# Splitting the gate stage's second product for pairs of tiles into seven matmuls of 256 columns

## The chip, the cores and the metric

One core of a Trainium2 chip runs the kernel. The metric is the device time of one execution in microseconds. The kernel before took 3012.85 us (median of three runs, 3011.78 to 3013.1).

## What is computed

The input x has 4 sequences of 2048 tokens with 512 channels, in float32. It is normalized per token (xn), and the output is x + attention(xn) + ffn(xn).

```
shifted = pad(xn)[:, :-1]                         # the token before
xr, xk, xv = mu * xn + (1 - mu) * shifted         # one mu for each
r, k, v = xr @ Wr.T, xk @ Wk.T, xv @ Wv.T
wkv = recurrence over the tokens of a sequence(k, v, w, u), stabilized by a running maximum
attention = (sigmoid(r) * wkv) @ Wo.T
hidden = silu(xn @ W1.T) * (xn @ W3.T)            # 2048 hidden channels
ffn = fwht(hidden) @ W2.T                         # Walsh-Hadamard transform along the hidden axis
```

## The kernel before

The 8192 tokens are worked through in 8 blocks of 1024 (`TB`), number i from 0 to 7. Each block goes through three stages on TensorE (PE): the projections of k, v and r; the gate stage ("up": W1 and W3, 16 tiles j of 128 hidden channels); and the down stage (W2 and Wo together, with the transform folded into W2 in block 0). The recurrence (`wkv`, line 333) runs on VectorE (DVE) and ScalarE (ACT) meanwhile. It is cut into ten pieces for each of four heads of 128 channels. Each call of `step()` issues one piece: ten pieces lie in the projections, and every gate tile from 1 to 15 issues two. So pieces 1 and 2 of a head lie in tiles 1, 6 and 11, pieces 3 and 4 in tiles 2, 7 and 12, and so on to pieces 9 and 10 in tiles 5, 10 and 15.

Products of 2 x 2 blocks are done with seven products instead of eight (the scheme of Strassen and Winograd): the weights are cut into gate and linear rows and two halves of the channels, the tokens into two halves of 512. The seven weight forms of a tile are numbered 0 to 6. Each product contracts 256 channels, so it is two matmuls of 128 x 128 weights with 512 columns. Form 0 meets the first quarter b11 of xn, and form 4 meets t1 = b12 - b11, the first of the sums. All sums, on both sides, are made beforehand (`token_forms`, line 409, and `forms_in`, line 469), the weight forms in blocks 0 and 1 only; they are then kept in DRAM (`part_w`) and loaded for each tile into a ring of three buffers.

In blocks 1 to 7 the gate tiles 1 to 15 are issued by `up_pairs` (line 668), which runs two generators side by side, one step of each in turn. `up_rest` (line 566) does one tile: products f1 (form 4 on t1), f2 (form 5), m21 (form 1), f3 (form 3), m22 (form 6) and f4 (form 2). PE accumulates in PSUM banks, and between the products ACT copies a bank into another that goes on from the same partial sum: pc from pb after f2, pd from pb after f3. The product f1 has a bank of its own, pf, which ACT copies into the buffer s5, in SBUF; DVE adds s5 to pb and pc (lines 606 and 608). The gate's nonlinearity is a tanh on ACT and two multiplications on DVE for each half of the tokens; for the second half they are the tail, which is issued in the middle of the next tile, after f2 and the copy into pc.

For tiles 4 to 15 the form 0 product is done for two tiles at once. Two tiles, two blocks of 128 channels and two quarters of 256 tokens make another 2 x 2, so `pair_product` (line 630) does seven matmuls of 256 columns where two tiles would have four of 512. It is run in the even tile two before its pair, in two banks a and b. Its matmuls, numbered by form, stand among the products of that tile like this: f1, P1, f2, P0, m21, P2, f3, P4 P5 P3, m22, P6, f4. ACT copies a part of one bank into the other between them (b<-a after P0, a<-b after P2, b<-b after P5) and the first product into `pair_s5`. At the end of the tile `out` (line 640) empties a and b into `pair_out`: ACT copies the lower 256 columns, DVE adds `pair_s5` to the upper ones. From `pair_out`, `fill` (line 559) copies twice, into the banks pb and pa of each tile of the pair; it does so one tile ahead, just before that earlier tile's f4.

What sets the order: every engine works its instructions in the order of the program (`InOrder`, line 26), and waits stand on its own queue. The eight banks are a queue in the gate stage: `take()` gives the one that has been free longest, `give()` appends. The order of the down stage is written out by hand (`down`, line 955). It starts with the banks that are free then, and uses the three of the last tile's tail, sorted by number, for another set; of these, ACT clears the third (`d0.clear("f")`, line 1018) once the tail has read it. The tail of tile 15 and the last pieces of the recurrence are issued in `before()`, line 1014. The first matmuls of the down stage are three groups of five with 256 columns.

Loads of weights are issued by SyncE (SP), in the order of the program. `normalize_early` (line 222) normalizes the next block during the gate stage, in three slots of 1024 columns in `pieces_w`.

Of the kernel before, what the change touches and what calls it, by code (L numbers as in the profile page):

```python
# [10 lines left out]
F32 = mybir.dt.float32  # L11
AF = mybir.ActivationFunctionType
ALU = mybir.AluOpType
# [3 lines left out]
P = 128  # L17
H = 512
TB = 2 * H
# [22 lines left out]
def tile_rwkv_attn_hadamard_ffn(  # L42
# [37 lines left out]
    down_w = dram.tile([2, 7, KH, P, QR, P], F32, name="down_w")  # L80
    deep_w = dram.tile([7, 7, P, QR, P], F32, name="deep_w")

    pair_w = dram.tile([NF // 2, P, 7, P], F32, name="pair_w")
    stat_d = dram.tile([n_blocks, 2, TB], F32, name="stat_d")
    xn_d = dram.tile([C, TB], F32, name="xn_d")

# [14 lines left out]
    def unit(j):  # L101
        return right[:, j // NP, j % NP, :]
# [20 lines left out]
    def take():  # L123
        return free_banks.popleft()

    def give(*pts):
        free_banks.extend(pts)
# [3 lines left out]
    tf_flat = tf.rearrange("p f k t -> p (f k t)")  # L131
    x_first, x_tok = (flat.rearrange("p (t c) -> p t c", c=C) for flat in (k_flat, tf_flat))

    pair_sums = k_sb[:, 0, :].rearrange("p (n t) -> p n t", n=4)
    pair_out = v_sb[:, 0, :].rearrange("p (n t) -> p n t", n=2)
    pair_s5 = unit(NF - 1)[:, 0 : H // 2]

    pair_forms = pieces_w[:, 7].rearrange("p q c -> p (q c)")[:, 0 : 4 * P].rearrange("p (f c) -> p f c", f=4)
    spread = v_sb[:, 0:2, :]
    stage = [v_sb[:, 2 + s // 2, ts(s % 2, H)] for s in range(4)]  # L140
    u2_of = [e1b[:, ts(g, H)] for g in range(KH)]
# [80 lines left out]
    def normalize_early(i):  # L222

        flat = pieces_w.rearrange("p u q c -> p (u q c)")
        both = flat[:, 0 : 2 * TB].rearrange("p (s t) -> p s t", t=TB)
        slots = [flat[:, ds((2 + n) * TB, TB)] for n in range(3)]

        def load(b):
            sp.dma_start(out=slots[b % 3], in_=xT[ts(b, P), ds(i * TB, TB)])

        load_spread(i, both)
        for b in range(3):
            load(b)
        yield
        for b in range(NB):
            xb = slots[b % 3]
            for s, op in ((0, ALU.mult), (1, ALU.add)):
                dve.tensor_tensor(xb, xb, both[:, s, :], op)
                if s:
                    sp.dma_start(out=xn_d[ts(b, P), :], in_=xb)  # L240
                    if b + 3 < NB:
                        load(b + 3)
                yield


# [215 lines left out]
    def seven_forms(t, a11, a12, a22, a21):  # L461

        sub = ALU.subtract
        pool.tensor_tensor(t[1], a21, a22, ALU.add)
        pool.tensor_tensor(t[2], t[1], a11, sub)
        pool.tensor_tensor(t[3], a12, t[2], sub)
        pool.tensor_tensor(t[0], a11, a21, sub)
# [4 lines left out]
    def load_parts(i, chunk):  # L472
        kind, n = chunk
        t = ring_a.tile([P, 7, KH, P], F32, tag="a", name=f"part_{i}_{kind}_{n}")
        if kind == "pair":
            sp.dma_start(out=t.rearrange("p f k c -> p (f k) c")[:, 0:7], in_=pair_w[n])
        elif kind == "rest":
            sp.dma_start(out=t[:, 1:7], in_=part_w[n][:, 1:7])
        elif is_first(i, n):
            sp.dma_start(out=t[:, 0:4], in_=wpart[n])  # L480
            forms_in(t)
        else:
            sp.dma_start(out=t, in_=part_w[n])
        return t

    def make_pair(p, w0, w1):
        (a11, a12), (a21, a22) = ([w[:, 0, b] for b in range(KH)] for w in (w0, w1))
        seven_forms([pair_forms[:, n] for n in range(4)], a11, a12, a22, a21)
        sp.dma_start(out=pair_w[p][:, 0:2], in_=w0[:, 0])
        sp.dma_start(out=pair_w[p][:, 2], in_=w1[:, 0, 1])  # L490

    def keep_pair(p):
        sp.dma_start(out=pair_w[p][:, 3:7], in_=pair_forms)

    def is_first(i, n):
        return i == (1 if n < 3 * KH else 0)
# [59 lines left out]

    def fill(row):

        pb, pa = take(), take()
        act.copy(pb, pair_out[:, row])
        act.copy(pa, pair_out[:, row])
        return pa, pb

    def up_rest(key, j, w, filled, tail, step, then):

        m11, m21, m22, f1, f2, f3, f4 = right_of["up"]
        h0, h1 = unit(j)[:, 0:H], unit(j)[:, H:TB]

        def product(pt, form, right, start=False):
            for b in range(KH):
                pe.matmul(
                    pt, lhsT=w[:, form, b, :], rhs=right[:, b, :], start=start and b == 0, stop=b == KH - 1,
                    skip_group_check=True,
                )

        if filled:
            pa, pb = filled
        else:  # L580
            pa, pb = take(), take()
            product(pa, 0, m11, True)
            act.copy(pb, pa)
        pf = take()
        product(pf, 4, f1, True)
        s5 = small.tile([P, H], F32, tag="s5", name=f"s5_{key}")
        act.copy(s5, pf)
        give(pf)
        yield
        product(pb, 5, f2)  # L590
        pc = take()
        act.copy(pc, pb)
        for f in tail:
            f()
        yield
        product(pa, 1, m21)
        act.activation(h0, pa, AF.Tanh, scale=0.5)
        yield
        product(pb, 3, f3)
        dve.scalar_tensor_tensor(h0, h0, 1.0, pa, ALU.add, ALU.mult)  # L600
        give(pa)
        pd = take()
        act.copy(pd, pb)
        yield
        step()
        dve.tensor_tensor(pb, pb, s5, ALU.add)
        product(pc, 6, m22)
        dve.tensor_tensor(pc, pc, s5, ALU.add)
        yield
        then()  # L610
        step()
        product(pd, 2, f4)
        yield (
            lambda: act.activation(h1, pc, AF.Tanh, scale=0.5),
            lambda: dve.tensor_tensor(h0, h0, pd, ALU.mult),
            lambda: dve.scalar_tensor_tensor(h1, h1, 1.0, pc, ALU.add, ALU.mult),
            lambda: dve.tensor_tensor(h1, h1, pb, ALU.mult),
            lambda: give(pd, pc, pb),
        )

    def pair_quarters():
        return [b11[:, b, cols] for b in range(KH) for cols in (lo, hi)]

    def make_pair_sums():
        q11, q12, q21, q22 = pair_quarters()
        t1, t2, t3, t4 = (pair_sums[:, n] for n in range(4))
        for out, x, y in ((t1, q12, q11), (t2, q22, t1), (t3, q22, q12), (t4, q21, t2)):
            difference(out, x, y)

    def pair_product(w):  # L630

        w = w.rearrange("p f k c -> p (f k) c")
        q11, _, q21, q22 = pair_quarters()
        t1, t2, t3, t4 = (pair_sums[:, n] for n in range(4))
        a, b = take(), take()

        def matmul(n, pt, right, start=False):
            pe.matmul(pt, lhsT=w[:, DEEP_AT[n]], rhs=right, start=start, stop=True, skip_group_check=True)

        def out(row, pt):  # L640
            act.copy(pair_out[:, row, lo], pt[:, lo])
            dve.tensor_tensor(pair_out[:, row, hi], pt[:, hi], pair_s5, ALU.add)


        matmul(1, a[:, hi], t1, True)
        act.copy(pair_s5, a[:, hi])
        yield
        matmul(0, a[:, lo], q11)
        act.copy(b[:, hi], a[:, lo])
        yield  # L650
        matmul(2, b[:, hi], t2)
        act.copy(a[:, hi], b[:, hi])
        yield
        matmul(4, a[:, lo], q21)
        matmul(5, b[:, hi], t3)
        act.copy(b[:, lo], b[:, hi])
        matmul(3, a[:, hi], q22)
        yield
        matmul(6, b[:, lo], t4)
        yield  # L660
        out(0, a)
        out(1, b)
        give(a, b)
        yield

# [1 line left out]

    def up_pairs(i, chunk, tail, step, beside):

        filled = None  # L670
        for j in range(1, NF):
            w = chunk(2 if j % 2 and j > 1 else 1)
            beside(j)
            ahead = []

            def fill_next():
                if 2 * FIRST_PAIR <= j + 1 < NF:
                    ahead.append(fill((j + 1) % 2))

            rest = up_rest(f"{i}_{j}", j, w, filled, tail, step, fill_next)  # L680
            product = iter(())
            for n in range(6):
                left = next(rest)
                if n == 0 and j % 2 == 0 and j + 2 < NF:
                    product = pair_product(chunk(0))
                next(product, None)
            tail, filled = left, ahead[0] if ahead else None
        return tail
# [546 lines left out]
    for i in range(n_blocks):  # L1235
# [34 lines left out]
        def chunk(more):  # L1270

            for _ in range(more):
                if loaded[0] < len(order):
                    parts.append(load_parts(i, order[loaded[0]]))
                    loaded[0] += 1
            return parts.pop(0)
# [70 lines left out]


        if i:
            make_pair_sums()  # L1350
            tail = up_pairs(i, chunk, tail, step, lambda j: staging(i, j))
        for j in range(NF if i == 0 else 0):
            if j % 2 and j > 2 * FIRST_PAIR:
# [95 lines left out]
```

## Time and profile before

| | |
|---|---|
| time, median of three | 3012.85 us |
| profiled execution, its own time | 3011.08 us |
| its span, first to last instruction | 3009.3 us |
| granted TensorE clock | 1.000 |
| gate stage of one block (1250 to 1430 us): busy PE, DVE, ACT | 180.0, 146.3, 93.0 of 180 us |
| DMA, mean over the span | 146 GB/s |

Busy time is the union of the instructions of an engine. The chain of waits follows the work that ended last back to its beginning; its pieces carry the start, the duration and the engine. In timelines each matmul of this kernel's program appears as two records, and a line such as "x12" merges twelve records of one kind; an idle time in front, and the engine that ended it, stand in brackets. Nearly all instructions carry line 36, that of `InOrder`, so they are told apart by their tiles: `right` holds the gate tiles and r, `part_rest` and `part_pair` are weights of the gate stage, `pieces_w` those of the down stage, `s` is s5, `v_sb` holds `pair_out`, `k_sb` the pair's sums, and `e`, `e1b`, `sa`, `sb` belong to the recurrence.

### The profile page before, as it was taken

The numbers are of one execution on the slowest core, as the hardware profiler recorded it, in microseconds if no ns is written. First come the engines' busy times: TensorE is split into PE (matmuls) and PEld (weight loads), VectorE is DVE, ScalarE is ACT, GpSimd is POOL, SyncE is SP. The second block draws the span as 40 slices with busy tenths as digits, with TensorE's granted clock in tenths as the row PEclk, the third lists the DMA queues.
The fourth block names the chain that finished last, engine by engine and source line by source line (L and its number), as shares of the span: only waits on it lengthen the run. The fifth ranks groups of instructions, "written<-read, shape, count | busy, mean of one in ns | idle before, by whom it ended". The sixth has DMA issues, their size and how long they took to land.

```text
span 3009.3 us, 26145 instructions
## 1 busy us (share of the span) xinstructions
PE 2993.2 (99%) x8954; PEld 1699.2 (56%) x8954; DVE 2428.0 (81%) x2637; ACT 1266.0 (42%) x2328; POOL 230.5 (8%) x220
## 2 busy tenths in 40 slices
PE   8999999999999999999999999999999999999999
PEld 3444444448644486445854558545585446844568
DVE  7688547789878897788977889778887788877887
ACT  4334134553345523554235542455425454144441
POOL 4264012220000000000000000000000000000000
PEclk9999999999999999999999999999999999999999
DMA  4266523666423374233633336332463324622244
GB/s 177 90 222 226 220 88 126 225 231 234 139 102 112 110 235 134 103 113 115 231 120 121 106 142 210 116 119 96 158 202 118 121 99 136 203 96 74 92 141 150
DMA packets 154979, 440.22 MB, mean 146 GB/s; under 512 B 16352, under 2 KB 36320, under 8 KB 152672
## 3 DMA queue, kind: packets, MB, share of 16 engines
q1 hardware_dynamic: 154560, 437.97, 42.6%
q8 instruction: 72, 1.18, 0.2%
q10 hardware_dynamic: 288, 0.59, 0.1%
q14 instruction: 59, 0.48, 0.0%
HBM read 363.01 MB, written 75.49 MB: 146 GB/s over the span
## 4 chain that ended last, share of the span: by engine, by line
PE 92%; DVE 7%; ACT 1%; DMA 0%; issue 0%; SPq 0%; DVEq 0%; ACTq 0%
PE bank L36 92%; DVE e1b L36 3%; DVE right L36 2%; DVE bank L36 1%; DVE e L36 1%; DVE v_sb L36 0%; ACT bank L36 0%; DMA xnT<-xT 0%; DVE sa L36 0%; ACT right L36 0%; DVE sb L36 0%; SPq L36 0%; DVE xnT L36 0%; DVE tf L36 0%; DVEq L1445 0%
## 5 line engine op out<-in xcount | busy, mean ns | idle before, releaser
L36 ACT COPY bank<-bank 128x512 f32<-128x512 f32 (+1 forms) x701 | 344.2, 491 | 999.1 <-PE bank L36 956.8
L36 PE MATMUL bank<-right,pieces_w 128*128 128x256 f32 (+1 forms) x2928 | 736.4, 409 | 2.9 <-ACT bank L36 2.9
L36 PEld LDWEIGHTS bank<-right,pieces_w 128*128 128x128 f32 x2928 | 555.1, 190 | 173.1 <-issue 99.2
L36 PE MATMUL bank<-tf,part_rest 128*128 128x512 f32 x1344 | 611.3, 592 | 1.6 <-ACT bank L36 1.6
L36 PEld LDWEIGHTS bank<-tf,part_rest 128*128 128x128 f32 x1344 | 255.1, 190 | 279.3 <-issue 248.3
L36 PE MATMUL bank<-right,part_full 128*128 128x512 f32 x840 | 369.6, 593 | 0.0
L36 DVE SCALAR_TENSOR_TENSOR right<-right,bank 128x512 f32<-128x512 f32 x256 | 175.1, 684 | 240.1 <-ACT right L36 239.4
L36 DVE TENSOR_TENSOR right<-right 128x1280 f32<-128x1280 f32 (+2 forms) x236 | 327.7, 1414 | 13.0 <-PE bank L36 12.0
L36 PE MATMUL bank<-tf,part_full 128*128 128x512 f32 x704 | 324.8, 592 | 0.0
L36 PE MATMUL bank<-xnT,part_rest 128*128 128x512 f32 x672 | 315.8, 592 | 0.0
L36 PEld LDWEIGHTS bank<-right,part_full 128*128 128x128 f32 x840 | 158.4, 190 | 203.2 <-issue 183.9
L36 ACT ACTIVATE right<-bank 128x512 f32<-128x512 f32 x308 | 184.1, 600 | 155.7 <-PE bank L36 110.2
L36 PE MATMUL bank<-xnT,part_full 128*128 128x512 f32 x528 | 248.1, 592 | 0.0
L36 PEld LDWEIGHTS bank<-tf,part_full 128*128 128x128 f32 x704 | 133.8, 190 | 159.4 <-issue 149.7
L36 DVE RECIPROCAL e1b<-e1b 128x512 f32<-128x512 f32 x64 | 213.9, 3343 | 0.0
L36 DVE TENSOR_TENSOR bank<-bank,s 128x512 f32<-128x512 f32 x256 | 168.2, 691 | 42.3 <-PE bank L36 29.8
L36 PEld LDWEIGHTS bank<-xnT,part_rest 128*128 128x128 f32 x672 | 127.7, 190 | 130.9 <-issue 117.2
L36 DVE TENSOR_TENSOR right<-right,bank 128x512 f32<-128x512 f32 x256 | 173.9, 679 | 6.5 <-PE bank L36 2.0
L36 PEld LDWEIGHTS bank<-xnT,part_full 128*128 128x128 f32 x528 | 100.3, 190 | 117.8 <-issue 113.3
L36 ACT COPY s<-bank 128x512 f32<-128x512 f32 x128 | 74.5, 582 | 214.0 <-PE bank L36 213.0
L36 PE MATMUL bank<-k_sb,pieces_w 128*128 128x256 f32 x630 | 146.3, 379 | 0.0
L36 DVE SCALAR_TENSOR_TENSOR right<-xnT,vec,right 128x1024 f32<-128x1024 f32 x92 | 121.9, 1355 | 21.3 <-ACT right L36 21.3
(137 smaller groups left out, 3160.3 us busy)
## 6 DMA issues: line engine op xcount, KB each, us to landing
pieces_w<-deep_w SPq DMA_DIRECT2D x343, 320.0 KB, 3.1
part_rest<-part_w SPq DMA_DIRECT2D x84, 768.0 KB, 4.3
part_full<-part_w SPq DMA_DIRECT2D x64, 896.0 KB, 4.6
part_w<-part_full SPq DMA_DIRECT2D x22, 896.0 KB, 6.7
part_pair<-pair_w SPq DMA_DIRECT2D x42, 448.0 KB, 4.1
pieces_w<-down_w SPq DMA_DIRECT2D x56, 320.0 KB, 4.7
deep_w<-pieces_w SPq DMA_DIRECT2D x7, 2240.0 KB, 8.6
tf<-x SPq DMA_DIRECT2D x7, 2048.0 KB, 7.9
```

What stands on the lines that cost most here:

```text
L36: return self.tc.keep_in_program_order(issue(*args, **kwargs))
```

## The change

In blocks 2 to 7 the form 4 product is done for pairs of tiles as well. `pair_product` gets a number: 0 is the product on b11 (form 0), run in the even tile as before, and 1 is the product on t1 (form 4), run in the odd tile just before its pair. Its results go not to `pair_out` but straight to the two s5 buffers of the coming pair, to which `up_rest` copied pf until now. For tiles 4 to 15 of these blocks `up_rest` issues no f1, takes no bank pf and makes no copy. Block 1 keeps f1.

Around it: the sums of t1's quarters are made by DVE at tile 2 of each block, into the place of tile 14. The weight forms of the second pair product are made by GpSimd (POOL) in block 0, beside those of the first, and kept in DRAM; in the other blocks SP loads them, at the even tile, into columns of `pieces_w` that were the third slot of `normalize_early`, which is left with two.

```diff
@@ normalize_early
-        slots = [flat[:, ds((2 + n) * TB, TB)] for n in range(3)]
+        slots = [flat[:, ds((2 + n) * TB, TB)] for n in range(2)]
...
@@ make_pair, keep_pair
-        (a11, a12), (a21, a22) = ([w[:, 0, b] for b in range(KH)] for w in (w0, w1))
-        seven_forms([pair_forms[:, n] for n in range(4)], a11, a12, a22, a21)
-        sp.dma_start(out=pair_w[p][:, 0:2], in_=w0[:, 0])
-        sp.dma_start(out=pair_w[p][:, 2], in_=w1[:, 0, 1])
+        for n, form in enumerate((0, 4)):
+            (a11, a12), (a21, a22) = ([w[:, form, b] for b in range(KH)] for w in (w0, w1))
+            seven_forms([pair_forms[n][:, m] for m in range(4)], a11, a12, a22, a21)
+            sp.dma_start(out=pair_w[n, p][:, 0:2], in_=w0[:, form])
+            sp.dma_start(out=pair_w[n, p][:, 2], in_=w1[:, form, 1])
...
-        sp.dma_start(out=pair_w[p][:, 3:7], in_=pair_forms)
+        for n in range(2):
+            sp.dma_start(out=pair_w[n, p][:, 3:7], in_=pair_forms[n])
@@ up_rest
-        pf = take()
-        product(pf, 4, f1, True)
-        s5 = small.tile([P, H], F32, tag="s5", name=f"s5_{key}")
-        act.copy(s5, pf)
-        give(pf)
+        if s5 is None:
+            pf = take()
+            product(pf, 4, f1, True)
+            s5 = small.tile([P, H], F32, tag="s5", name=f"s5_{key}")
+            act.copy(s5, pf)
+            give(pf)
@@ pair_product
-        def out(row, pt):
-            act.copy(pair_out[:, row, lo], pt[:, lo])
-            dve.tensor_tensor(pair_out[:, row, hi], pt[:, hi], pair_s5, ALU.add)
+        def out(slot, pt):
+            act.copy(slot[:, lo], pt[:, lo])
+            dve.tensor_tensor(slot[:, hi], pt[:, hi], s5, ALU.add)
...
-        out(0, a)
-        out(1, b)
+        for slot, pt in zip(outs(), (a, b)):
+            out(slot, pt)
@@ up_pairs
+            if i >= 2 and j == 2:
+                make_pair_sums(1)
...
+            def new_s5():
+                s5_pair[:] = [small.tile([P, H], F32, tag="s5", name=f"s5_{i}_{2 * pair + row}") for row in range(2)]
+                return s5_pair
...
+            both = i >= 2 and pair >= FIRST_PAIR
...
-                if n == 0 and j % 2 == 0 and j + 2 < NF:
-                    product = pair_product(chunk(0))
+                if n == 0 and pair >= FIRST_PAIR and 2 * pair < NF:
+                    if j % 2 == 0:
+                        product = pair_product(0, chunk(0).rearrange("p f k c -> p (f k) c"), kept)
+                        if both:
+                            sp.dma_start(out=pair_w1, in_=pair_w[1, pair])
+                    elif both:
+                        product = pair_product(1, pair_w1, new_s5)
```

More of the change, by code (lines that the diff above doesn't have):

```diff
@@ L81, in tile_rwkv_attn_hadamard_ffn @@
     deep_w = dram.tile([7, 7, P, QR, P], F32, name="deep_w")
-    pair_w = dram.tile([NF // 2, P, 7, P], F32, name="pair_w")
+    pair_w = dram.tile([2, NF // 2, P, 7, P], F32, name="pair_w")
     stat_d = dram.tile([n_blocks, 2, TB], F32, name="stat_d")
@@ L132, in tile_rwkv_attn_hadamard_ffn @@
     x_first, x_tok = (flat.rearrange("p (t c) -> p t c", c=C) for flat in (k_flat, tf_flat))
-    pair_sums = k_sb[:, 0, :].rearrange("p (n t) -> p n t", n=4)
+    pair_sums = [t.rearrange("p (n t) -> p n t", n=4) for t in (k_sb[:, 0, :], unit(NF - 2))]
     pair_out = v_sb[:, 0, :].rearrange("p (n t) -> p n t", n=2)
-    pair_s5 = unit(NF - 1)[:, 0 : H // 2]
-    pair_forms = pieces_w[:, 7].rearrange("p q c -> p (q c)")[:, 0 : 4 * P].rearrange("p (f c) -> p f c", f=4)
+    pair_s5 = [unit(NF - 1)[:, ts(n, H // 2)] for n in range(2)]
+    pair_w1 = pieces_w.rearrange("p u q c -> p (u q c)")[:, ds(4 * TB, 7 * P)].rearrange("p (f c) -> p f c", f=7)
+    pair_forms = [
+        t[:, 0 : 4 * P].rearrange("p (f c) -> p f c", f=4)
+        for t in (pieces_w[:, 7].rearrange("p q c -> p (q c)"), k_sb[:, 0, :])
+    ]
     spread = v_sb[:, 0:2, :]
@@ L225, in normalize_early @@
         both = flat[:, 0 : 2 * TB].rearrange("p (s t) -> p s t", t=TB)
-        slots = [flat[:, ds((2 + n) * TB, TB)] for n in range(3)]
+        slots = [flat[:, ds((2 + n) * TB, TB)] for n in range(2)]
         def load(b):
-            sp.dma_start(out=slots[b % 3], in_=xT[ts(b, P), ds(i * TB, TB)])
+            sp.dma_start(out=slots[b % 2], in_=xT[ts(b, P), ds(i * TB, TB)])
         load_spread(i, both)
-        for b in range(3):
+        for b in range(2):
             load(b)
@@ L235, in normalize_early @@
         for b in range(NB):
-            xb = slots[b % 3]
+            xb = slots[b % 2]
             for s, op in ((0, ALU.mult), (1, ALU.add)):
@@ L240, in normalize_early @@
                     sp.dma_start(out=xn_d[ts(b, P), :], in_=xb)
-                    if b + 3 < NB:
-                        load(b + 3)
+                    if b + 2 < NB:
+                        load(b + 2)
                 yield
@@ L475, in load_parts @@
         if kind == "pair":
-            sp.dma_start(out=t.rearrange("p f k c -> p (f k) c")[:, 0:7], in_=pair_w[n])
+            sp.dma_start(out=t.rearrange("p f k c -> p (f k) c")[:, 0:7], in_=pair_w[0, n])
         elif kind == "rest":
@@ L564, in fill, with up_rest @@
         return pa, pb
-    def up_rest(key, j, w, filled, tail, step, then):
+    def up_rest(key, j, w, filled, s5, tail, step, then):
         m11, m21, m22, f1, f2, f3, f4 = right_of["up"]
@@ L619, in up_rest, with pair_quarters, make_pair_sums, pair_product @@
         )
[L621 to L626, printed above, removed]
+    def pair_quarters(n):
+        return [(b11, t1)[n][:, b, cols] for b in range(KH) for cols in (lo, hi)]
+    def make_pair_sums(n):
+        q11, q12, q21, q22 = pair_quarters(n)
+        t1, t2, t3, t4 = (pair_sums[n][:, m] for m in range(4))
         for out, x, y in ((t1, q12, q11), (t2, q22, t1), (t3, q22, q12), (t4, q21, t2)):
             difference(out, x, y)
[L630 to L634, printed above, removed]
+    def pair_product(which, w, outs):
+        q11, _, q21, q22 = pair_quarters(which)
+        t1, t2, t3, t4 = (pair_sums[which][:, m] for m in range(4))
+        s5 = pair_s5[which]
         a, b = take(), take()
@@ L638, in matmul @@
             pe.matmul(pt, lhsT=w[:, DEEP_AT[n]], rhs=right, start=start, stop=True, skip_group_check=True)
-        def out(row, pt):
-            act.copy(pair_out[:, row, lo], pt[:, lo])
-            dve.tensor_tensor(pair_out[:, row, hi], pt[:, hi], pair_s5, ALU.add)
+        def out(slot, pt):
+            act.copy(slot[:, lo], pt[:, lo])
+            dve.tensor_tensor(slot[:, hi], pt[:, hi], s5, ALU.add)
         matmul(1, a[:, hi], t1, True)
-        act.copy(pair_s5, a[:, hi])
+        act.copy(s5, a[:, hi])
         yield
@@ L668, in up_pairs, with kept @@
     def up_pairs(i, chunk, tail, step, beside):
-        filled = None
+        filled, s5_pair = None, [None, None]
+        def kept():
+            return [pair_out[:, row] for row in range(2)]
         for j in range(1, NF):
@@ L673, in up_pairs @@
             beside(j)
-            ahead = []
+            if i >= 2 and j == 2:
+                make_pair_sums(1)
+            ahead, pair = [], j // 2 + 1
             def fill_next():
@@ L678, in fill_next @@
                     ahead.append(fill((j + 1) % 2))
-            rest = up_rest(f"{i}_{j}", j, w, filled, tail, step, fill_next)
+            def new_s5():
+                s5_pair[:] = [small.tile([P, H], F32, tag="s5", name=f"s5_{i}_{2 * pair + row}") for row in range(2)]
+                return s5_pair
+            rest = up_rest(f"{i}_{j}", j, w, filled, s5_pair[j % 2], tail, step, fill_next)
             product = iter(())
+            both = i >= 2 and pair >= FIRST_PAIR
             for n in range(6):
                 left = next(rest)
-                if n == 0 and j % 2 == 0 and j + 2 < NF:
-                    product = pair_product(chunk(0))
+                if n == 0 and pair >= FIRST_PAIR and 2 * pair < NF:
[5 more added lines that the diff above has]
+                        product = pair_product(1, pair_w1, new_s5)
                 next(product, None)
@@ L1349, in tile_rwkv_attn_hadamard_ffn @@
         if i:
-            make_pair_sums()
+            make_pair_sums(0)
             tail = up_pairs(i, chunk, tail, step, lambda j: staging(i, j))
```

## The prediction, made before the change was run

> **What bounds the kernel now.** I read the shares of busy time and the chain first, then the chain in order of time, then the timelines of TensorE (PE), VectorE (DVE) and ScalarE (ACT) over one block, 1242 to 1440 us. (Blocks 1 to 7 repeat every 368.6 us: the chain shows the same sequence at 1038.84, 1407.41 and 1775.98.)
>
> ```profile
> PE 2993.2 (99%) x8954; PEld 1699.2 (56%) x8954; DVE 2428.0 (81%) x2637; ACT 1266.0 (42%) x2328; POOL 230.5 (8%) x220
> ...
> PE 92%; DVE 7%; ACT 1%; DMA 0%; issue 0%; SPq 0%; DVEq 0%; ACTq 0%
> ```
>
> PE has no idle time to win; less PE work is the only way to go faster. But the chain spends 24 us per block on DVE:
>
> ```profile
> 1407.41 0.57 ACT bank L36
> 1407.98 0.52 ACT right L36
> 1408.53 0.70 DVE right L36
> ...
> 1430.80 0.66 ACT bank L36 x2
> 1431.50 344.46 PE bank L36 x1072
> ```
>
> ```profile
> 1424.38 6.79 PE L36 MATMUL bank<-right,pieces_w 128*128 128x256 f32 x30
> 1431.50 2.43 PE L36 MATMUL bank<-right,pieces_w 128*128 128x256 f32 x10 [0.33 <-ACT bank L36]
> ```
>
> Here, where the gate stage ends and the down stage starts, PE waits, although only 0.33 us: DVE runs without a gap from 1408.53 to there, finishing the last head of the recurrence. So PE and DVE are both at their limit at the end of each block, and PE work taken out in front of this point returns as waiting.
>
> **The gain.** The timeline shows each of the program's matmuls as two records, so starts give the price:
>
> ```profile
> 1365.12 0.59 PE L36 MATMUL bank<-k_sb,part_pair 128*128 128x256 f32 x2
> 1365.56 0.59 PE L36 MATMUL bank<-xnT,part_pair 128*128 128x256 f32 x2
> ...
> 1368.14 5.31 PE L36 MATMUL bank<-tf,part_rest 128*128 128x512 f32 x12
> 1373.29 1.88 PE L36 MATMUL bank<-xnT,part_rest 128*128 128x512 f32 x4
> ```
>
> 256 columns take 0.43 us, 512 columns 5.15/6 = 0.858 us. A pair loses four of 512 (3.43 us) and gains seven of 256 (3.01): 0.42 us less. Blocks 2 to 7 have six such pairs each: 36 x 0.42 = 15.2 us. A rule speaks against this: the Trainium skill, "TensorE: Matmul & The Clock Gate", section "Back-to-back issue gap", gives streams of weight load and matmul about 81 ns at 128 columns and 131 ns at 512, so narrow matmuls cost more than their share. Drawn straight between, 256 columns would cost 0.75 of 512 (an estimate from that page), and a pair 7 x 0.64 - 3.43 = +1.05 us, 38 us in all. The row has exactly half, with the weight load (190 ns) beside it, so I take the row.
>
> **What is added elsewhere.** ACT, per pair: two copies of 512 go (2 x 0.58), six of 256 come (6 x 0.37): +1.1 us, on an engine 52% busy in this stage (93 of 180 us). DVE: two additions of 256 per pair (2 x 0.41), and four differences per block (1.7 us), which lie in the 3.4 us that DVE idles early in tile 2 (before 1265.57). SP: one load of 448 KB more per pair, 0.32 us to issue, 4.1 us to land, issued a tile (11.6 us) ahead and behind a part load that has to wait for the tile's start anyhow: nothing. Normalizing ahead with two slots instead of three: a load now waits for the store from its slot, but is needed five tiles (58 us) later: nothing; were that cover gone, some 5 us of DVE per block. Block 0: POOL makes 24 forms more, 2.6 us per pair (rows of 1.11, 0.60, 0.46, 0.45), and SP issues three stores more per pair; POOL is at most 67% busy there, and forms are made two tiles ahead: 0, at most 2 us in all.
>
> **Middle of the block: a wait that moves.** Without the first-sum product a tile is, on PE: P1, f2, P0, m21, P2, f3, P4 P5 P3, m22, P6, f4 = 11.6 us, where each P is one pair matmul of 256 columns, and each other name a product of two matmuls of 512. A tile's start is now where the previous f4 ends, and f2 ends 2.15 us later, instead of 3.43 or more. After f2 ACT has, in this order, the copy into pc, the tanh of the last tile, and the copy b<-a that P2 needs:
>
> ```profile
> 1384.27 0.57 ACT L36 COPY bank<-bank 128x512 f32<-128x512 f32 x1 [1.34 <-PE bank L36]
> 1384.76 0.60 ACT L36 ACTIVATE right<-bank 128x512 f32<-128x512 f32 x1
> 1385.24 0.39 ACT L36 COPY bank<-bank 128x256 f32<-128x256 f32 x1
> ```
>
> These take 1.36 us (1384.27 to 1385.63), and P2 comes 2.15 us after f2's end: the copy into pc may start at most 2.9 us into the tile. In every pair tile after the change pc is the bank that the pair product of the tile before calls b, and the copy waits for the DVE addition that empties it. That addition stands behind the tile's two pieces of recurrence. The trace has this case with its whole length, in tile 10 (f4 ends at 1369.86), whose pieces are the two longest:
>
> ```profile
> 1363.98 3.34 DVE L36 RECIPROCAL e1b<-e1b 128x512 f32<-128x512 f32 x1
> ...
> 1373.17 0.75 DVE L36 TENSOR_TENSOR v_sb<-bank,right 128x256 f32<-128x256 f32 x2
> ```
>
> It ends at 1373.92, 4.06 us into the next tile. Before, tile 11 had no pair product, so only ACT waited (1.32 us, with the tanh behind it). After: pc copy at 4.17, b<-a done at 5.53, P2 at 5.59 instead of 4.29: 1.3 us of PE idle. Tiles 5 and 10 carry these pieces, so tiles 6 and 11 pay; tile 9 now also has additions, which adds about 0.1 in tile 10 and 0.1 in tile 11. Elsewhere, by the same walk: after the pieces of tiles 3 and 8 the addition ends at 2.5, after 4 at 2.7, after the light ones at 1.3 to 2.2: no stall. Sum 1.3 + 0.1 + 1.4 = 2.8 us per block, 16.8 in six. Bounds: 2.0 to 3.6 per block (12 to 22), as the 2.9 limit is missed or met by 0.1 to 0.2 in four tiles.
>
> **End of the block.** From the end of m21 of tile 13 (1398.62) to the resume at 1431.50 the trace takes 32.88 us; PE could have resumed after 15 products of two matmuls of 512, 25.74, and 15 matmuls of 256, 6.45: 32.2. So 0.68 us are lost before (by starts; the idle of 0.33 is counted from the modelled end). After: two first-sum products (14 and 15) go, 3.43, and P2 to P6 of tile 13's new product come, 2.15: PE is ready at 30.9. DVE has no such relief: its order from tile 13's gate multiplication on is the same, plus tile 13's two additions, 0.67: its last operation ends 33.9 us after m21 (before: 1432.08 - 1398.62 = 33.46; 0.67 more, and 0.2 of waiting goes). And PE waits for a later one of its operations. ACT must clear a bank of the last tile before the copy that frees PE:
>
> ```profile
> 1430.08 0.68 DVE L36 TENSOR_TENSOR right<-right,bank 128x512 f32<-128x512 f32 x1
> 1430.68 0.68 DVE L36 SCALAR_TENSOR_TENSOR right<-right,bank 128x512 f32<-128x512 f32 x1
> 1431.39 0.69 DVE L36 TENSOR_TENSOR right<-right,bank 128x512 f32<-128x512 f32 x1
> ```
>
> Before, it is the bank read by the first of these three (ended 1430.76, clear at 1430.80). It is the last by number of the tail's three banks, and the new rotation makes it the bank of the third row in five blocks and of the second in one. From the end of that operation to PE the trace has 0.74. So PE resumes at 33.9 + 0.74 = 34.7: idle 3.8, loss 3.1 us; in the one block 2.4. In all 5 x 3.1 + 2.4 = 17.9 us. Bounds per block: 1.8, if the clear waited for the first of the three rows as before, to 3.8, the whole idle: 11 to 23.
>
> **Sum.** -15.2 + 16.8 + 17.9 = +19.5 us. The profiled execution took 3011.08 us (span 3009.3), 1.8 us under the median of 3012.85; I add the difference to the median: 3032. Range of this case from the bounds: -15 + 12 + 11 = +8 to -15 + 22 + 23 + 2 = +32: 3021 to 3045.
>
> **Rivals.**
> - The full gain arrives, 2998 us: PE stays without gaps. For it: PE 99% busy, ACT 52%, DVE 81% in the stage (146 of 180 us from 1250 to 1430). Against: at the end of each block PE already waits for DVE, and this cannot hold unless DVE's last operation came 3 us earlier relative to PE. Decisive is a single point, the resume after the first three down products; if its idle stays at 0.33 us and P2 never waits, this rival is right. 0.07.
> - Only one of the two places pays. Block ends alone: -15.2 + 17.9, 3016; P2 alone: -15.2 + 16.8, 3014. For the first: the pc copy could find its bank empty earlier if DVE gets ahead. Both give a time that nothing tells from no change. 0.15.
> - Dearer than I count: a stall in more tiles (the 2.5 to 2.7 cases pass the 2.9 limit by little), or narrow matmuls that cost more beside 512-column neighbours: 0.3 us in eight more tiles per block gives +14, 3046. The rows show no such price. 0.10.
> - The likeliest, 3032 (3021 to 3045): 0.68.
>
> A measurement of this kernel tells about 0.2% (6 us) from no change. Faster by more: 0.08; within: 0.14; slower: 0.78. To hold 8 in 10 the range takes in the likeliest case and most of the second: 3013 to 3043.
>
> **What would show it.** After: PE idle "<-ACT bank" in front of P2 in tiles 6 and 11 of blocks 2 to 7, about 1.3 us; ACT's pc copy waiting for DVE there, on `s` or `v_sb`; an idle of some 3.5 us at the first down product that resumes, preceded in the chain by DVE's recurrence; block 1 unchanged, blocks 2 to 7 some 3.2 us longer each. I am wrong if the blocks get shorter, if idle stands in front of f2 or m22 (ACT's fill), or if PE shows no idle but matmuls of 256 start more than 0.43 us apart.

## The result and the profile after

The changed kernel took 3038.48 us (median of four runs, 3037.04 to 3038.61), against 3012.97 for the kernel before: a ratio of 1.0084, with a 95% interval of 1.007 to 1.0099. One of the four runs of the kernel before that were taken beside it is a slow one of 6501.43 us, whose cause is not known: the ratio leaves it out, and the other three took 3011.78 to 3013.1. The predicted 3032 us is 6.5 us short, and the time lies in the range of 3013 to 3043. The profiled execution took 3038.53 us, its span 3036.6.

The page of the changed kernel, first the busy time of the engines (share of the span, number of instructions), then the chain by engine:

```profile
PE 2987.4 (98%) x9170; PEld 1736.4 (57%) x9170; DVE 2464.3 (81%) x2733; ACT 1293.5 (43%) x2472; POOL 251.9 (8%) x244
...
PE 80%; DVE 18%; ACT 2%; issue 0%; DMA 0%; ACTq 0%; DVEq 0%
```

PE is busy for 5.8 us less and the span is 27.3 us longer. (Busy time is no measure of the work taken out: a start that is late without an idle counts as busy.) In the chain DVE rose from 7 to 18%: PE now waits for it more often. One group of the page shows the same (busy, mean ns, idle in front and its releaser), before and after. It holds the down products on `right`, and after the change the second pair product's matmuls on t1's sums too, since these lie in `right` and their weights in `pieces_w`:

```profile
L36 PE MATMUL bank<-right,pieces_w 128*128 128x256 f32 (+1 forms) x2928 | 736.4, 409 | 2.9 <-ACT bank L36 2.9
```

```profile
L36 PE MATMUL bank<-right,pieces_w 128*128 128x256 f32 (+1 forms) x3216 | 824.0, 407 | 26.9 <-ACT bank L36 26.9
```

The chain of the changed kernel over one block, in order of time (start, duration):

```profile
1434.94 1.23 DVE e L36
1436.16 1.21 DVE bank L36 x2
1437.37 1.13 DVE right L36
1438.53 2.43 DVE right L36 x3
1441.68 230.44 PE bank L36 x780
...
1685.27 3.26 DVE e1b L36
...
1693.23 1.22 DVE right L36
1696.63 35.37 PE bank L36 x102
```

Before, PE carried the chain from one block end to the next (344 us in one piece). Now it goes over to DVE in the middle as well, and PE resumes at 1696.63. What PE does there, in its timeline (in brackets the idle in front, and what ended it):

```profile
1691.41 1.88 PE L36 MATMUL bank<-tf,part_rest 128*128 128x512 f32 x4
1693.12 0.59 PE L36 MATMUL bank<-xnT,part_pair 128*128 128x256 f32 x2
1693.55 1.88 PE L36 MATMUL bank<-xnT,part_rest 128*128 128x512 f32 x4
1696.63 0.70 PE L36 MATMUL bank<-k_sb,part_pair 128*128 128x256 f32 x2 [1.19 <-ACT bank L36]
1697.16 1.88 PE L36 MATMUL bank<-tf,part_rest 128*128 128x512 f32 x4
```

This is tile 6: f2, P0, m21, and then P2, which was due at 1693.55 + 1.72 = 1695.27 and starts 1.36 us late. The step after it takes 0.53 us instead of 0.43. The cause stands in the timelines of DVE and ACT:

```profile
1693.23 1.22 DVE L36 SCALAR_TENSOR_TENSOR right<-right,e1b 128x1024 f32<-128x1024 f32 x1
1694.38 0.75 DVE L36 TENSOR_TENSOR s<-bank,right 128x256 f32<-128x256 f32 x2
```

```profile
1695.21 0.57 ACT L36 COPY bank<-bank 128x512 f32<-128x512 f32 x1 [2.40 <-DVE s L36]
1695.69 0.60 ACT L36 ACTIVATE right<-bank 128x512 f32<-128x512 f32 x1
1696.18 0.39 ACT L36 COPY bank<-bank 128x256 f32<-128x256 f32 x1
```

The copy into pc waits 2.40 us for the DVE additions that empty tile 5's pair banks; these stand behind piece 10 of the recurrence, whose last operation starts at 1693.23. The tanh and b<-a follow, and only then P2. Tile 11 has the same, with v_sb in the place of s (ACT waits 3.23 us there) and the same 1.19 us of idle on PE.

The end of the block, PE first, then ACT, then DVE's three tail rows:

```profile
1804.35 4.48 PE L36 MATMUL bank<-right,pieces_w 128*128 128x256 f32 x20
1810.43 2.42 PE L36 MATMUL bank<-right,pieces_w 128*128 128x256 f32 x10 [1.60 <-ACT bank L36]
1814.51 2.43 PE L36 MATMUL bank<-right,pieces_w 128*128 128x256 f32 x10 [1.65 <-ACT bank L36]
```

```profile
1809.51 0.60 ACT L36 ACTIVATE right<-bank 128x512 f32<-128x512 f32 x1 [6.91 <-DVE bank L36]
1810.00 0.38 ACT L36 COPY bank<-bank 128x256 f32<-128x256 f32 x1
1813.81 0.39 ACT L36 ACTIVATE bank<-had_sb 128x256 f32<-128x256 f32 x1 [3.43 <-DVE right L36]
```

```profile
1811.77 0.68 DVE L36 TENSOR_TENSOR right<-right,bank 128x512 f32<-128x512 f32 x1
1812.37 0.68 DVE L36 SCALAR_TENSOR_TENSOR right<-right,bank 128x512 f32<-128x512 f32 x1
1813.08 0.69 DVE L36 TENSOR_TENSOR right<-right,bank 128x512 f32<-128x512 f32 x1
```

PE waits twice. The third group of the down stage waits for a copy on ACT behind the tanh, which waits for DVE's addition to pc; the fourth waits for the copy behind the clear, and the clear for the third tail row (until 1813.77), not the first.

**Where the 27.3 us of span lie.** I compared each start of a matmul on PE with the one before it plus 0.43 us per record of 512 columns or 0.216 per record of 256; what is over is lost time, whether or not the trace calls it idle. The table sums it for one block (us; the losses of under 0.1 us in the projections, equal in both, are left out):

| one block | before | after |
|---|---|---|
| P2 in tiles 6 and 11, with the slow step behind it | 0 | 2.92 |
| other small losses in the gate stage (0.07 to 0.11 each, eight of them) | 0 | 0.77 |
| end of the block | 0.75 | 3.78 |
| length of the block | 368.57 | 372.83 |

From the rows: 2.92 + 0.77 + 3.03 - 6 x 0.42 = +4.2 us, and the block is 4.26 us longer. Five blocks are like this, and one (block 3) is 3.53 us longer, with 0.93 us in place of the last 1.65. Block 1, which has no second pair product, is 0.76 us longer. The rest, 1.65 us, lies before PE's first product of the span (16.64 us before, 18.29 after). Of it 1.1 us are PE's wait for its first load, 6.5 us before and 7.6 after. Whether that is the change's is open: this wait was 6.5 us in three and 7.7 in one of the four profiled kernels that make no second set of forms, and 6.5 to 8.1 in the ten that do, over 7.3 in eight of them.

### The profile page after: what moved, and what is told of

Read it like the earlier page. It is cut to its first block, busy times and chain, and to the rows that moved or that the text cites. A ratio compares the mean times of both kernels' runs of the same rounds, so it can differ in the third digit from the quotient of the medians.

```text
span 3036.6 us, 26959 instructions
## 1 busy us (share of the span) xinstructions
PE 2987.4 (98%) x9170; PEld 1736.4 (57%) x9170; DVE 2464.3 (81%) x2733; ACT 1293.5 (43%) x2472; POOL 251.9 (8%) x244
## 4 chain that ended last, share of the span: by engine, by line
PE 80%; DVE 18%; ACT 2%; issue 0%; DMA 0%; ACTq 0%; DVEq 0%
PE bank L36 80%; DVE e1b L36 6%; DVE right L36 5%; DVE bank L36 2%; DVE e L36 2%; DVE v_sb L36 1%; DVE sa L36 1%; ACT right L36 1%; ACT bank L36 1%; DVE sb L36 1%; DVE s L36 0%; DMA right<-w 0%; DVE carry L36 0%; DVE xnT L36 0%; ACTq L36 0%
## 5 line engine op out<-in xcount | busy, mean ns | idle before, releaser
L36 PE MATMUL bank<-right,pieces_w 128*128 128x256 f32 (+1 forms) x3216 | 824.0, 407 | 26.9 <-ACT bank L36 26.9
L36 ACT COPY bank<-bank 128x512 f32<-128x512 f32 (+1 forms) x809 | 384.3, 475 | 1042.9 <-PE bank L36 949.5
L36 PEld LDWEIGHTS bank<-right,pieces_w 128*128 128x128 f32 x3216 | 608.8, 190 | 254.5 <-issue 132.0
L36 PE MATMUL bank<-tf,part_rest 128*128 128x512 f32 x1056 | 491.6, 592 | 2.4 <-ACT bank L36 2.4
L36 PEld LDWEIGHTS bank<-tf,part_rest 128*128 128x128 f32 x1056 | 200.4, 190 | 172.8 <-issue 149.2
L36 PE MATMUL bank<-tf,pieces_w 128*128 128x256 f32 (+1 forms) x490 | 142.2, 409 | 1.0 <-DVE tf L36 1.0
```

Source lines behind the costliest of these rows:

```text
L36: return self.tc.keep_in_program_order(issue(*args, **kwargs))
```

## The experiments

The theory: two waits that are independent of each other eat the gain, (a) the pair banks' additions behind a recurrence piece, 6 x 2.8 us, and (b) the end of the block, of which the bank of the clear is a part. The rivals: the narrow matmuls are no faster at all; the additional loads, stores and sums cost something; or an end of the block that waits for DVE takes whatever is won in front of it.

**One: the additions earlier.** In `pair_product`; ACT's copies stay where they were.

```diff
-        for slot, pt in zip(outs(), (a, b)):
-            out(slot, pt)
+        slots = outs()
+        for slot, pt in zip(slots, (a, b)):
+            dve.tensor_tensor(slot[:, hi], pt[:, hi], s5, ALU.add)
+        yield
+        for slot, pt in zip(slots, (a, b)):
+            act.copy(slot[:, lo], pt[:, lo])
@@ fill_next
+                next(product, None)
```

> In the changed kernel the two DVE additions that empty a and b are issued ahead of the tile's second recurrence piece instead of behind it; all else is the same work. If P2 in tiles 6 and 11 waits for these additions by way of the pc copy, its two stalls (1.36 us each in the trace, and 0.1 us of slow restart) vanish: 6 x 3.0 = 18 us, 1 to 2 more from small restarts in other tiles, so about 3019 us, with the stall at the end of the block unchanged (PE resumes 34.6 us after m21 of tile 13). If the time is lost to dearer narrow matmuls, to ACT's total work or to the added loads, the order of two additions changes nothing: 3038 us.

Measured: 3021.31 us (3020.37 to 3022.29), ratio 1.0027 (1.0017 to 1.0038). Its DVE timeline, in the place that answers to 1693 above, has the additions ahead of piece 10:

```profile
1684.43 0.75 DVE L36 TENSOR_TENSOR s<-bank,right 128x256 f32<-128x256 f32 x2
1685.09 1.21 DVE L36 SCALAR_TENSOR_TENSOR right<-right,e 128x1024 f32<-128x1024 f32 x1
1686.34 1.23 DVE L36 SCALAR_TENSOR_TENSOR right<-right,e1b 128x1024 f32<-128x1024 f32 x1
```

```profile
1683.94 1.88 PE L36 MATMUL bank<-tf,part_rest 128*128 128x512 f32 x4
1685.91 0.70 PE L36 MATMUL bank<-xnT,part_pair 128*128 128x256 f32 x2
1686.44 1.88 PE L36 MATMUL bank<-xnT,part_rest 128*128 128x512 f32 x4
```

Here P0, not P2, comes 0.25 us late and no bracket marks it: ACT's copies of the pair product and of its first product (1684.88 to 1685.86 in ACT's timeline) come just too late: P0 starts 0.05 us after the last of them. (ACT waited 4.09 us for the additions, which now stand ahead of these copies in the program.) The P2 waits are gone, the two waits at the end of the block are as before this edit (1.60 and 1.65 us), and the time fell by 17.2 us. Wait (a) is shown, and the end of the block did not take the gain back.

The 17.2 us are not all P2's. A block from 2 to 7 is 2.43 us shorter (370.39 for 372.83), not 3.0 or more as expected, since P0 is late now: 14.6 us in six. Another 2.4 us lie in block 1, which has no second pair product. There f3 waited in three tiles, and waits in one now (0.50 us by starts for 2.88 in sum). It is a wait of the same kind, since f3 goes on in pb, which the copy into pc has to read first: in the kernel before, in one of these tiles, that copy waits 3.04 us for the additions that empty the pair banks (at 612.29 in ACT's timeline).

**Two: the clear's bank.** The tail's banks are handed to `down` in a fixed order, so that the third of them, which is cleared, is always the one that the tail reads first.

```diff
@@ up_rest
+        last_tail[:] = (pb, pc, pd)
@@ down
-        late = [pt for pt in banks if not any(pt is b for b in early)]
+        late = list(last_tail)
```

> In the changed kernel the tail's three banks are handed to the down stage in a fixed order, so that the bank cleared before PE may go on is the one that the tail reads first. If the number of that bank costs what was predicted, five blocks win 1.3 us each and one 0.65: 7 us, and up to 0.7 in block 1; about 3031 us. If the chain of the recurrence on DVE alone sets the end and the clear is beside it: 3038 us.

Measured: 3030.77 us (3029.84 to 3032.22), ratio 1.0059 (1.0046 to 1.0072). The fall of 7.7 us stands beside an expected 5 x 1.3 + 0.65 = 7.15. In the trace the fourth group's idle is 0.33 us instead of 1.65, and the third group's is still 1.61.

**Three: both.**

> Both edits together. If the two places are independent: 3038.5 - 19 - 7 = 3012 us, no difference from the kernel before. What is then left of the loss is DVE's chain at the block's end (some 1.8 us per block more than before). If one place only hides the other: 3019 us or more.

Measured: 3013.53 us (3011.76 to 3014.69), ratio 1.0001 (0.9993 to 1.001). The two repairs add up: 17.2 + 7.7 = 24.9, and together they bring 25.0. What is left in PE's timeline of one block, by starts: 1.26 us in the middle and, at the end, 2.47, in these two lines:

```profile
1797.81 2.43 PE L36 MATMUL bank<-right,pieces_w 128*128 128x256 f32 x10 [1.60 <-ACT bank L36]
1800.57 2.43 PE L36 MATMUL bank<-right,pieces_w 128*128 128x256 f32 x10 [0.33 <-ACT bank L36]
```

That is 3.73 against the kernel before's 0.75: 2.98 more, less the 2.53 that the pairs save, +0.45. The block is 369.08 us long, +0.51. The gain is there, and the end of the block and the small losses take it.

**Four: everything but the product.** The forms, the stores, the loads of `pair_w1`, the sums of t1 and the two slots stay; the second pair product is not issued, so every tile has its f1 again.

```diff
-                    elif both:
-                        product = pair_product(1, pair_w1, new_s5)
```

> The changed kernel without its second pair product: f1 stays in every tile, but the second set of forms is made and stored in block 0, loaded in blocks 2 to 7, the sums of t1 are made, and the normalization ahead has two slots. If all these are hidden, as predicted: 3013 us, within 1. If transfers, POOL or the smaller ring of slots cost something, it shows here alone: 3018 to 3030 us.

Measured: 3013.8 us (3012.16 to 3015.84), ratio 1.0002 (0.9994 to 1.001). The transfers and sums cost nothing that can be measured, which leaves room for some 3 us at most (the end of the interval).

**Five and six: a piece of the recurrence moved forward.** What is left at the end is DVE's work behind the last tiles. An eleventh piece in the projections takes one from tile 15; five is on top of both repairs, six on the kernel before.

```diff
-                    if hooks[0] in (5, 6, 8, 10, 11, 12, 13, 14, 15, 17):
+                    if hooks[0] in (5, 6, 8, 10, 11, 12, 13, 14, 15, 16, 17):
```

> Both repairs (the additions ahead of the tile's second piece, the clear's bank read by the first tail row) and, beside them, one more recurrence piece in the projections, so that each gate tile does the piece that it did one place later before and tile 15 has only the last piece. My theory: what is left at the end of the block (1.6 + 0.34 us of idle TensorE and its slow restarts, some 2.4 a block) is VectorE's chain behind tile 15's two pieces; with one piece of about 5.7 us less there, VectorE is ahead of TensorE and the idle goes: 3013.5 - 6 x 2.4 = about 2999 us, range 2996 to 3003. Rival: VectorE has no slack in the projections or in another tile, and the piece that is moved forward makes it late there: 3008 us or more.

> The kernel before with only the piece moved forward. If the split's gain is real (36 pairs of 0.42 us) and is hidden in the runs so far by the end of the block, this one can only win back the 0.68 us that the kernel before loses at the end of each block: 7 x 0.68 = 4.8, about 3008 us (3006 to 3012), and the run with both repairs and the piece is 9 to 13 us below it. Rival: the split by itself is worth nothing, and the piece alone makes the difference: both runs equal within 2 us.

Measured: five 3008.89 us (3007.74 to 3010.76), ratio 0.9987 (0.998 to 0.9993); six 3012.66 us (3010.44 to 3014.43), ratio 0.9999 (0.999 to 1.0007). Neither theory nor rival: five is 10 us above what I expected, and six won nothing. In five the end fell from 2.47 to 0.77 us, but the middle rose from 1.26 to 2.25. ACT's timeline and then PE's, at the start of tile 4:

```profile
1653.13 1.06 ACT L36 ACTIVATE k_sb<-k_sb 128x1024 f32<-128x1024 f32 x1
1654.09 2.13 ACT L36 ACTIVATE e<-e 128x1024 f32<-128x1024 f32 x2
1656.13 1.09 ACT L36 COPY bank<-v_sb 128x512 f32<-128x512 f32 x2
```

```profile
1655.87 0.59 PE L36 MATMUL bank<-k_sb,part_pair 128*128 128x256 f32 x2
1656.76 1.98 PE L36 MATMUL bank<-tf,part_rest 128*128 128x512 f32 x4 [0.30 <-ACT bank L36]
```

An odd number of pieces makes the pieces change places in each tile. Piece 6, with 4.2 us of activations, now stands ahead of `fill`'s copies (bank<-v_sb) in tiles 3, 8 and 13, and f2 of the next tile waits for them. It is the wait in front of f2 of which the prediction said that it would prove it wrong; the changed kernel doesn't have it in blocks 2 to 7, this order has.

**Seven and eight: two pieces forward,** so that the places are restored; the second at the ninth of 18 steps.

```diff
-                    if hooks[0] in (5, 6, 8, 10, 11, 12, 13, 14, 15, 17):
+                    if hooks[0] in (5, 6, 8, 9, 10, 11, 12, 13, 14, 15, 16, 17):
```

> Both repairs and two more recurrence pieces in the projections, so that each gate tile has the same kind of pieces in the same places as with both repairs alone and tile 15 has none. In the run with one piece forward the end of the block fell to 0.8 us, but the even and the odd pieces changed places in every tile, and 2.2 us a block came up in the middle, where ScalarE's copies that fill the next tile's banks lie behind a piece's activations. My theory: with the places restored the middle is what it was with both repairs alone (1.3 us a block) and the end is gone: 3013.5 - 6 x 2.5 = about 2999 us, range 2996 to 3004. Rival: VectorE, busy 84 to 91 us of the 97 in the projections, has no room for a second piece of about 5 us there, TensorE waits in the projections, and the time is 3008 us or more.

> The kernel before with the same two pieces moved forward. It can win back only its own 0.7 us at the end of each block: 3008 to 3012 us. If the split's gain is real, the run with both repairs and the two pieces is some 10 us below this one (36 pairs x 0.42 less what the middle still loses, 6 x 1.3); if the split is worth nothing, or its waits are only moved, the two are equal within 3 us.

Measured: seven 3009.86 us (3008.25 to 3012.12), ratio 0.999 (0.9983 to 0.9997); eight 3019.03 us (3018.12 to 3020.34), ratio 1.0019 (1.0012 to 1.0027). In seven the end is free of loss and the middle has 1.2 to 1.5 us, as expected; PE waits in the projections, and there the rival is right, but not its engine. (The 84 to 91 of 97 us that the expectation quotes for the projections are of the down stage, so this number was no argument; from 1529 to 1629, mostly the projections, DVE was busy 79 of 100 us.) ACT is late, for one step:

```profile
1578.03 1.13 ACT L36 ACTIVATE right<-xnT,omm 128x1024 f32<-128x1024 f32 x1
1579.07 1.04 ACT L36 ACTIVATE e1b<-e1b 128x1024 f32<-128x1024 f32 x1
1580.01 1.04 ACT L36 ACTIVATE sb<-sb 128x1024 f32<-128x1024 f32 x1
1580.96 0.57 ACT L36 COPY bank<-bank 128x512 f32<-128x512 f32 x1
```

```profile
1581.59 1.98 PE L36 MATMUL bank<-pieces_w,part_full 128*128 128x512 f32 x4 [1.10 <-ACT bank L36]
```

The piece's exponentials (e1b, sb) meet the token mixing of r (right<-xnT,omm), and the copy that PE needs lies behind them. Eight has the same 1.10 us at the same place, and is 7 us above the range expected. Seven is 9.2 us below eight, near the 10 that were expected if the split's gain is real.

**Nine and ten: the second piece elsewhere,** in nine at the last of the 18 steps, in ten at the end of gate tile 1, each with both repairs.

```diff
@@ nine
+                    if hooks[0] in (5, 6, 8, 10, 11, 12, 13, 14, 15, 16, 17, 18):
@@ ten: the steps of five, and in up_pairs
+                if j == 1 and n == 5:
+                    step()
```

> Both repairs, with the two additional pieces behind the last two projections' steps (16 and 18 of 18), so that none meets the token mixing on ScalarE that cost 1.3 us a block when the second piece lay in the fourth projection. My theory: the places in the gate tiles are those of both repairs alone (middle 1.3 us a block), the end and the projections are free of idle: 3013.5 - 6 x 2.5 = about 2999 us. Rival: the last projections have no room on VectorE, and what was 1.6 us a block in the fourth comes up there: 3008 to 3012 us.

> Both repairs and one piece forward, with the second additional piece at the end of gate tile 1, where ScalarE is idle for 2.5 us and VectorE for 4.6 us soon after. My theory: as the run beside it, about 2999 us. Rival: in tiles 1 and 2 the banks come free later, and the time is 3006 to 3010 us.

Measured: nine 2997.69 us (2997.27 to 2998.72), ratio 0.9951 (0.9938 to 0.9963); ten 2997.01 us (2996.94 to 2998.02), ratio 0.9949 (0.9935 to 0.9962). Both beat both kernels. Page lines of nine, to be read beside those of the changed kernel:

```profile
PE 2981.3 (100%) x9170; PEld 1739.1 (58%) x9170; DVE 2466.2 (82%) x2733; ACT 1295.4 (43%) x2472; POOL 249.3 (8%) x244
...
PE 95%; DVE 4%; ACT 1%; issue 0%; DMA 0%; ACTq 0%; DVEq 0%
...
L36 PE MATMUL bank<-right,pieces_w 128*128 128x256 f32 (+1 forms) x3216 | 819.1, 406 | 0.0
```

The same number of instructions on PE and DVE, 26.9 us of idle in that group gone. By starts, a block loses 1.24 us in the middle and nothing at the end.

**Eleven and twelve: the pieces without the repairs,** on the kernel before and on the changed kernel, with the steps of nine.

> The kernel before with the two pieces behind the last two projections' steps, nothing else. Of the 15.2 us that the best version gains, this tells the pieces' share: my theory is that the kernel before can win only the 0.68 us at the end of its blocks (it lost 2.4 us of TensorE in all): 3008 to 3012 us, so the split is worth 36 pairs of 0.42 us once its waits are gone. Rival: the pieces alone bring most of it, under 3003 us.

> The changed kernel with the two pieces, without the two repairs. My theory: the places in the gate tiles stay (each tile has the pieces of the tile after it before), so the two long pieces now lie in tiles 4 and 9 and the third quarter's wait of 1.4 us moves to tiles 5 and 10: 3.5 us a block stay, the end (3.05 a block and what of it the clear's bank brings) goes, as VectorE is early there: 2997.5 + 6 x (3.5 - 1.3) = about 3011 us (3008 to 3016). Rival: without the repair of the clear's bank the end of the block still waits some 1.3 us: about 3019 us.

Measured: eleven 3007.5 us (3006.75 to 3008.81), ratio 0.9982 (0.9974 to 0.9989); twelve 3014.96 us (3013.7 to 3017.07), ratio 1.0006 (0.9998 to 1.0014). Eleven is just under the range expected. Twelve has no idle at the end, with the clear on the late bank, and the P2 waits have moved one tile forward, to tiles 5 and 10:

```profile
1677.03 0.70 PE L36 MATMUL bank<-right,pieces_w 128*128 128x256 f32 x2 [1.20 <-ACT bank L36]
...
1736.91 0.70 PE L36 MATMUL bank<-k_sb,part_pair 128*128 128x256 f32 x2 [1.20 <-ACT bank L36]
```

So the clear's bank costs something only while DVE is late, and the P2 waits follow pieces 9 and 10. Eleven tells the split from the pieces. Here are two tiles without a wait, from P1 of tile 6 to P1 of tile 8, in PE's timeline of eleven and then of nine:

```profile
1679.18 0.59 PE L36 MATMUL bank<-k_sb,part_pair 128*128 128x256 f32 x2
...
1702.81 0.59 PE L36 MATMUL bank<-k_sb,part_pair 128*128 128x256 f32 x2
```

```profile
1674.93 0.59 PE L36 MATMUL bank<-k_sb,part_pair 128*128 128x256 f32 x2
...
1698.21 0.59 PE L36 MATMUL bank<-k_sb,part_pair 128*128 128x256 f32 x2
```

23.63 us for two tiles against 23.28, of which 0.06 is a late start at 1689.18: 0.41 us less, as the sum had it. Over a block, 367.82 against 366.61 us: the split brings 1.2 us net there, 7.3 us in six blocks, and the 1.24 us that the middle still loses is the other half of it. Nine is 9.8 us below eleven. The rest is mostly block 1: eleven loses 3.9 us there at four starts, nine 0.5. Runs one and two tell which of the two repairs does that: in block 1 the starts of f3 lose 0.5 us with the early additions, and 3.0 with the clear's bank alone. The repairs were not run on the kernel before, which loses 2.1 us at these starts, so what block 1 wins must not be put down to the split.

## Why the prediction was right, and what was off

- **The gain, 36 x 0.42 = 15.2 us: right.** Nine against eleven has 0.41 us per pair, where nothing waits. The estimate from the Trainium skill, "TensorE: Matmul & The Clock Gate", "Back-to-back issue gap", would have made the pairs 38 us dearer; no run here shows that, the measured row holds. The whole 15.2 us arrive in no run: with the waits at the end gone, the late starts in the middle still take half of them, and 7.3 us are left.
- **P2 in tiles 6 and 11: place and cause right, size short.** Said were 1.3 + 0.1 + 1.4 = 2.8 us a block. Each of the two waits is 1.36 us by starts, plus a step of 0.53 instead of 0.43 us behind it: 2.92. That is nearly the sum. What failed is "no stall" elsewhere: eight starts are 0.07 to 0.11 us late, 0.77 us a block. The walk through the tiles had set them at zero, with "missed or met by 0.1 to 0.2 in four tiles" kept only for the bounds. All in all 3.7 us for 2.8: 5.3 us of the 6.5 that the prediction is short. The upper bound given, 3.6, was too low as well.
- **The end of the block: 3.1 said, 3.03 measured,** and 2.3 in the one block for 2.4. From the end of m21 of tile 13 (1779.88) to the resume it takes 34.63 us for 34.7. The text put it all at one resume; it lies in two waits, as the third down group waits too. Undoing the clear's bank brought 7.7 us for 7.15.
- **"Everything else 0": right** for loads, stores and sums (run four). Block 1 was said to be unchanged and is 0.76 us longer: three waits in front of f3, behind ACT's copy into pc, were there before (0.60, 1.01 and 0.51 us by starts) and are now 1.13, 0.89 and 0.86. Run four, without the second pair product, has them too (1.45, 0.60 and 0.96), so they come with the rest of the change; with what part of it was not tried.
- **The rivals.** The full gain, 2998, was given 0.07 because DVE's last operation would have to come 3 us earlier relative to PE. Runs nine and ten do that, by taking two pieces from behind the last tiles, and reach 2997 to 2998 us; the agreement with 2998 is partly chance, since they also win the kernel before's own 0.75 us at each end and its block 1, and lose 1.24 us a block. "Dearer than I count", small stalls in more tiles, was right in kind (0.77 us a block for the 2.4 it assumed).

## What to carry to other kernels

PE work that is taken out is worth only what the other engines' order lets through: walk each wait that the shorter distance brings nearer, and count the starts that are late by a tenth, not only those that the trace calls idle. An instruction that frees a bank belongs ahead of long work on its queue, and a bank that others wait for should be one that is read first; here these two repairs were worth 25 us, and no instruction was added. Moving work off the crowded end of a stage pays, but where it lands decides: the same two pieces were worth 3.7 us over the repairs alone in one place and 16 us in another.

## What the runs showed of the hardware

After each wait of PE the next step was longer than its like: 0.53 us for 0.43 behind a pair matmul, 2.26 for 2.16 behind a group of ten (1814.51 to 1816.77 in the changed kernel), in every kernel here that waits at these places. So a wait cost some 0.27 us more by starts than the idle in its bracket: 1.36 and 0.10 against 1.19. (Some 0.17 us of these are a matter of the view, which counts the idle from the modelled end of the matmul before, here 1695.44 for a due start of 1695.27.) And a start can be 0.1 to 0.26 us late with no bracket at all, as P0 in run one.
